# Aggregation in a written order for three engines, and three more units of it with split products

## The chip, the cores and the metric

The kernel runs on one core of a Trainium2 chip. The metric is device time in microseconds (us) from one execution; the time given for a kernel is the median of its runs. Engines are named as in the profile: PE is TensorE (matmuls; PEld its weight loads), DVE is VectorE, ACT is ScalarE, POOL is GpSimd, SP is SyncE. DMAs are issued from the queues of SP, ACT and POOL.

## The reference, cut to what matters

Two graph layers over N = 4096 nodes with D = 512 features, all in float32, one after the other:

```
bw, ba = sign(w0), max(sign(x), 0)
x  = layernorm(x + relu(adj @ (ba @ bw.T)))          # layer 0

h  = x @ edge_w
e  = where(adj > 0, h @ h.T, -9e15)
edge_att = softmax(e, axis=1)
node_att = softmax(x @ node_w, axis=0)
x  = layernorm(x + (adj * node_att * edge_att) @ (x @ w1) + bias)   # layer 1
```

## The kernel before, in words

The work runs in four stages, one after the other on PE.

**Layer 0** (from 0 to about 508 us) multiplies each block of 128 rows of `adj`, split into a high and a low part (`hi` on ACT, `lo` on DVE), with a packed product. The function `rest` then finishes one row block on DVE in steps that the main loop calls between the parts of the next row block. Every second row block, `rest` calls `left`, which combines two row blocks `low` and `high` of the new x into the seven left operands of a Strassen product and stores them in DRAM as `lop_d`, for the last stage.

**h and scores** (about 508 to 1075 us) compute `h` and `h @ h.T`, mask the scores, write them to DRAM as `s_d` and keep row minima and sums for the softmax.

**Aggregation** (from about 1075 us to the end) is where nearly all of the change lies. The product of the weighted attention with x is cut into 4 x 4 units `Aggregate(g, r)`: g is the block of output columns (1024 nodes), r the block of 1024 nodes that is summed over. A unit is one Strassen product: seven products m of a left operand (loaded from `lop_d`) with a right operand. The right operands are made of four tiles of 128 x 2048 elements: for each tile n the unit issues a load of the scores (`load`, POOL queue) and of `adj` (`mask`, POOL queue), then `shift` (DVE), `exp` (ACT), `clip` of adj (ACT), `weigh` (DVE, scores times adj), and after all four tiles four sums `combine` (DVE). Thirteen buffers of 1 MB (`slot`, `lent`) hold all of these; the list `free` gives them out.

One product m is either whole (two sums of 4 matmuls of 128 x 512 columns) or split once more into seven inner products (14 matmuls of 128 x 256 columns). Split are the three products m in `SPLIT` of the units for which `in_two(n)` holds, n = 4 to 14. The right operands of the inner products are made on DVE by `second` (four operations of 128 x 512 elements for a product) into one buffer, `extra[0]`; the left ones are made by `lefts` during the units n = 0 to 3 from the loaded `lop`, stored in DRAM as `lop2_d` from the ACT queue, and loaded by the later units in four DMAs for a product. Each sum lives in SBUF (`sums`) between units: ACT copies it into a PSUM bank (`seed`) and back (`evict`); there are six banks. At the end of a group g, `join_inner` and `join` (DVE) combine the products, and `Finish` multiplies them with w1 on PE (`po`, line 1244), adds them to x on DVE (line 1255), normalises and stores. The finishing of group g runs between the products of group g + 1, from the list `todo`, one entry for every 6 units of matmul work.

What sets the order of the aggregation: each unit has a list `steps()` of actions with a fraction of the unit of before it, at which an action is recorded. DVE's, ACT's and PE's instructions are then ordered by the scheduler of the programming layer, except those that are pinned with `keep_in_program_order`:

```python
    (0.53, lambda: (self.exp(2), self.shift(3))),
    (0.61, lambda: self.exp(3)),
    (0.63, lambda: self.clip(2)),
```

w1 is loaded into `w1_s` (line 1391, SP queue) before unit 0, and four DVE subtractions (`t3`, `r12`, `t2`, `t4`; line 1420) prepare it.

**The tail** (about 1901 us to the end) finishes the last group: `Finish` for its two halves, interleaved.

Of the kernel before, what the change touches and what calls it, by code (L numbers as in the profile page):

```python
# [11 lines left out]
F32 = mybir.dt.float32  # L12
# [12 lines left out]
SPLIT = 6, 4, 3  # L25
# [4 lines left out]
def kernel(  # L30
# [49 lines left out]

    lop2_d = [dram.tile([P, len(SPLIT), 4, BG // 2, P], F32, name=f"lop2_d{g}") for g in range(HG)]

# [76 lines left out]
    with (  # L159
# [153 lines left out]
        def rest(n, b, xb, acc, before):  # L313
# [4 lines left out]
            scr = wp.tile([P, D], F32, name="scr", tag="scr")  # L318
            nc.vector.scalar_tensor_tensor(xb, acc, 0.0, xb, ALU.max, ALU.add)
# [13 lines left out]
            if n % 2:  # L333
                left(n // 2, before, xb)
            yield
            transpose_rows(b, xb)

# [110 lines left out]
        def between_h(q, n):  # L448
            count[0] += q is None
            if q is None and count[0] % 14 in (8, 10, 13) and ahead_h:  # L450
                next(ahead_h.popleft())
            if q is None and count[0] > 6 and count[0] % 5 % 2 == 0:
                premask(nc.sync, 0, 3)
# [349 lines left out]
    panels = {}  # L803

    least = {}
# [6 lines left out]
    def panel(A):  # L812

        cols = slice(A * BG, (A + 1) * BG)
        nm = least.pop(A)
        pt = banks.popleft() if banks else ps_tr.tile([P, W], F32, name="ptm", tag="tr")
# [17 lines left out]
        d = small.tile([P, BG, NG], F32, name="d")  # L834
        nc.vector.tensor_tensor(d, nm.unsqueeze(2).to_broadcast([P, BG, NG]), nmax_c[:, cols, :], ALU.subtract)
        nc.scalar.activation(d, d, AF.Exp)
        nc.vector.tensor_mul(d, d, sum_c[:, cols, :])
        f = pan.tile([P, BG], F32, name="f")
# [4 lines left out]


    pinned = [tc.keep_in_program_order]

    class Aggregate:
# [58 lines left out]
        def steps(self):  # L906

            self.q, self.a, self.since = [None] * 4, [None] * 4, [None] * 8

            def begin():  # L910
                for n in range(2):
                    self.load(n)
                    self.mask(n)

            return [
                (0.0, begin),
                (0.14, lambda: self.load(2)),
                (0.15, lambda: self.shift(0)),
                (0.22, lambda: self.shift(1)),
                (0.25, lambda: self.exp(0)),  # L920
                (0.27, lambda: self.clip(0)),
                (0.28, lambda: self.load(3)),
                (0.30, lambda: self.exp(1)),
                (0.34, lambda: self.clip(1)),
                (0.36, lambda: self.weigh(0, 2, True)),
                (0.42, lambda: self.shift(2)),
                (0.47, lambda: self.weigh(1, 3, True)),
                (0.53, lambda: (self.exp(2), self.shift(3))),
                (0.61, lambda: self.exp(3)),
                (0.63, lambda: self.clip(2)),  # L930
                (0.68, lambda: self.weigh(2, None, True)),
                (0.71, lambda: self.clip(3)),
                (0.75, lambda: self.weigh(3, None, True)),
                *((0.8 + 0.05 * n, lambda n=n: self.combine(n)) for n in range(4)),
            ]

        def early_steps(self):
# [14 lines left out]
            for n in range(2):  # L952
                g = 2 * self.g + n
                yield lambda g=g: not rest[g], lambda g=g: (lowest(g), panel(g))
# [32 lines left out]
        def second(self, m):  # L987

            h, w = BG // 2, W // 2
            r = self.right(m)  # L990
            (r11, r12), (r21, r22) = [[r[:, k : k + h, c : c + w] for c in (0, w)] for k in (0, h)]
            t2, t3, t4 = (extra[0][:, n, :].rearrange("p (b w) -> p b w", w=w) for n in range(3))
            self.halves = r11, r21, r22, t4, r12, t2, t3
            nc.vector.tensor_sub(t3, r22, r12)
            nc.vector.tensor_sub(r12, r12, r11)
            yield
            nc.vector.tensor_sub(t2, r22, r12)
            nc.vector.tensor_sub(t4, r21, t2)
            yield

        def lefts(self, m, lop):

            (l11, l21), (l12, l22) = [[lop[:, k : k + 2, f : f + P] for f in (0, P)] for k in (0, BG // 2)]
            s = [rows.tile([P, 2, BG // 2, P], F32, name="left2", tag="rows") for _ in range(2)]
            s4, s3, s2, s1 = (x[:, n] for x in s for n in range(2))

            tc.keep_in_program_order(nc.vector.tensor_add(s1, l21, l22))
            tc.keep_in_program_order(nc.vector.tensor_sub(s2, s1, l11))
            tc.keep_in_program_order(nc.vector.tensor_sub(s3, l11, l21))  # L1009
            tc.keep_in_program_order(nc.vector.tensor_sub(s4, l12, s2))  # L1010
            to = lop2_d[self.r][:, SPLIT.index(m)]
            yield
            for n in range(2):
                nc.scalar.dma_start(to[:, ts(n, 2)], s[n])
# [5 lines left out]
        def main(self, between, two):  # L1020
            uses = deque(u for u in plan if u.unit is self)
            whole = sum(u.work for u in uses)
            halves = (None for m in [u.m for u in uses if u.ns and u.ns[0] == 1] for _ in self.second(m))
            stores = deque()
            past = 0
            while plan and plan[0].unit is self:
                u = plan.popleft()
                u.seed()
# [6 lines left out]
                if stores:  # L1035
                    next(stores.popleft(), None)
                if not u.ns:
                    next(halves, None)
                if u.end:
                    free.append(self.right(u.m))  # L1040
                    if not self.g and u.m in SPLIT:
                        stores.append(self.lefts(u.m, lops["lop"]))
                        next(stores[0])
                between(past / whole, u.work)
            if stores:
                next(stores.popleft(), None)
# [13 lines left out]
    class Sums:  # L1060
# [3 lines left out]
        lefts = 0, 1, 2, 6, 5, 4, 3  # L1064

        def __init__(self, unit, m, h=0, more=False, keep=False, ns=None):
# [5 lines left out]
            self.bank = None  # L1072

# [4 lines left out]
        def seed(self):  # L1078
# [8 lines left out]
            if self.unit.r:  # L1087
                assert self.ns or not any(m == self.m for m, _ in [*inner, *inner_next])
                nc.scalar.copy(self.bank[:, : self.w], self.to())  # L1089
            elif self.w < W:  # L1090
                nc.vector.memset(self.bank[:, : self.w], 0.0)

        def multiply(self):
            r, m = self.unit.r, self.m
            if self.begin and not self.ns:
                lops["lop"] = lopp.tile([P, BG, HD], F32, name="lop")
                nc.sync.dma_start(lops["lop"], lop_d[r][:, m])
            elif self.begin:
                low, high = (lopp.tile([P, 4, BG // 2, P], F32, name="lop2", tag="lop") for _ in range(2))
                raw, s = lop_d[r][:, m], lop2_d[r][:, SPLIT.index(m)]  # L1100
                nc.sync.dma_start(low[:, :2].rearrange("p n b f -> p (n b) f"), raw[:, :, :P])
                nc.sync.dma_start(low[:, 2:], s[:, :2])
                nc.sync.dma_start(high[:, :2], s[:, 2:])
                nc.sync.dma_start(high[:, 2], raw[:, BG // 2 :, P:])
                lops["low"], lops["high"] = low, high
            if self.ns:
                products = []
                for k, n in enumerate(self.ns):
                    at = self.lefts[n]
                    lop = lops["high"][:, at - 4] if at > 3 else lops["low"][:, at]  # L1110
# [3 lines left out]
            start = not r and self.w == W  # L1114
            for ps, lop, rop, K in products:
                for k in range(K):
                    nc.tensor.matmul(ps, lop[:, k, :], rop[:, k, :], start=start, stop=(k == K - 1), skip_group_check=True)  # L1117
                    start = False
            if self.keep:
                kept.append(self.bank)  # L1120

        def evict(self):
            u = self.unit
            if not self.keep:
                assert u.r or not self.ns or not any(m == self.m for m, _ in [*inner, *inner_next])
                nc.scalar.copy(self.to(), self.bank[:, : self.w])  # L1126
                banks.append(self.bank)
            if self.end and self.ns and (u.r == HG - 1 or blocks.index(u) == len(blocks) - 2):
                inner_next.extend((self.m, n) for n in range(7))
# [20 lines left out]
    def join_inner(g, m, n):  # L1150
# [4 lines left out]
        m1, m6, m7 = both[:, :w], both[:, w:], part(g, m, (6,))  # L1155
        out_, a, b = (
            (c11, m1, c11),
# [3 lines left out]
            (c22, m7, c22),  # L1161
            (c12, m6, c12),
            (c21, m7, c21),
        )[n]
        nc.vector.tensor_add(out_, a, b)

    def join(g, n, engine):
# [12 lines left out]
        engine.tensor_tensor(out_, a, b, op)  # L1180

    spare = []

    class Finish:

# [6 lines left out]
        def steps(self, then):  # L1192

            for q in range(2):
                yield from self.pair(q, ps_tr)
                some = q, q + 2
                yield lambda some=some: self.norm(some)
                yield lambda some=some: (self.scale(some), then and then.load(some))
# [12 lines left out]
        def pair(self, q, pool):  # L1211
# [6 lines left out]
            def combine():  # L1218
# [10 lines left out]
                nc.vector.tensor_sub(s2, l21, l11)  # L1229

            def multiply(name, lop, rop, *to):
# [11 lines left out]
                for k in range(KD // 2):  # L1243
# [7 lines left out]
                    )  # L1251
                f, _ = panels[self.A]
                for i, h in to:
                    xb = self.xbs[i][:, ts(h, HD)]
                    nc.vector.scalar_tensor_tensor(xb, po, f[:, i : i + 1], xb, ALU.mult, ALU.add)

# [10 lines left out]

            yield combine
            yield lambda: multiply("y", l11, 0, (a, 0))
            yield lambda: (multiply("x", l12, 1, (a, 0)), half_stats(a, 0))  # L1270
            yield lambda: multiply("y", 1, 5, (a, 1))
            yield lambda: (multiply("z", 0, 4, (b, 1)), nc.vector.tensor_sub(l12, l12, s[1]))
            yield lambda: (multiply("y", 2, 6, (b, 1)), half_stats(b, 1))
            yield lambda: (multiply("z", 3, 2, (a, 1)), half_stats(a, 1))
# [218 lines left out]
```

## Time and profile before

| | |
|---|---|
| median of 3 runs | 1931.44 us (1930.81 to 1933.38) |
| profiled execution, own time | 1934.05 us |
| its span, first to last instruction | 1932.3 us |
| PE busy | 1913.5 us, 99% of the span |
| DVE busy | 1387.0 us, 72% |
| ACT busy | 1024.3 us, 53% |
| POOL busy | 280.5 us, 15% |
| DMA | 508.72 MB, mean 263 GB/s |

Shares of busy time are averages over the stages; the stages have different limits, and a stretch of time is read by itself. In groups of instructions each row gives the line, engine, operation, output and inputs with their shape, the count, the busy time, the mean of one instruction in ns, and the idle time of the engine just ahead of it with what ended it. A matmul in float32 leaves two records in the trace.

### The profile page before, as it was taken

To read this page: it belongs to the slowest core of one execution; us is meant where nothing else is said; L and a number is where in the kernel's file an instruction comes from. 1 tells how busy PE (TensorE), PEld (TensorE's weight loads), DVE (VectorE), ACT (ScalarE), POOL (GpSimd) and SP (SyncE) were. 2 spreads that over 40 slices of the span, in tenths; PEclk is the share of its full clock that TensorE was granted. 3 is DMA by queue.
4 is the path that set the end of the run, shared out by engine and by line. 5 is a ranking of instruction groups with operands and counts; after the bars stand their busy time and mean duration, and the time that the engine had idled before them with its cause. 6 is when DMAs were issued, how large, how long until landed. Compare 5 with 4: busy or idle time off the path is not lost.

```text
span 1932.3 us, 20169 instructions
## 1 busy us (share of the span) xinstructions
PE 1913.5 (99%) x6708; PEld 1200.9 (62%) x6708; DVE 1387.0 (72%) x2058; ACT 1024.3 (53%) x1619; POOL 280.5 (15%) x409
## 2 busy tenths in 40 slices
PE   8999999999999999999999999999999999999998
PEld 6888888888644455444555444456666666666655
DVE  6766676666765567566664986687869987798746
ACT  5433333333202567576777665546767577757731
POOL 0122122222321101011111111111101101111100
PEclk9999999999999999999999999999999999999999
DMA  8888888888585478577773998787778787887731
GB/s 311 285 328 308 306 311 307 328 308 292 176 280 198 157 259 312 188 276 253 294 301 113 347 327 285 271 283 246 259 266 292 259 279 260 301 283 258 274 109 44
DMA packets 169527, 508.72 MB, mean 263 GB/s; under 512 B 15696, under 2 KB 41040, under 8 KB 161744
## 3 DMA queue, kind: packets, MB, share of 16 engines
q1 hardware_dynamic: 89472, 226.39, 34.6%
q0 software_dynamic: 64688, 239.10, 33.1%
q10 hardware_dynamic: 15264, 41.95, 6.0%
q8 instruction: 53, 0.87, 0.2%
q14 instruction: 50, 0.41, 0.1%
HBM read 385.74 MB, written 121.63 MB: 263 GB/s over the span
## 4 chain that ended last, share of the span: by engine, by line
PE 90%; DVE 4%; DMA 2%; issue 2%; ACT 1%; POOL 0%; ACTq 0%; DVEq 0%; POOLq 0%
PE bank L1117 33%; PE seven L749 14%; PE acc L395 11%; PE acc L396 11%; PE pe L676 6%; PE seven L101 5%; PE po L1244 3%; PE pt L638 3%; DMA slot<-s_d 1%; PE pt L355 1%; PE acc L236 1%; PE acc L235 1%; PE pw L213 1%; DMA over<-in_w_dram 1%; PE bank L1244 0%
## 5 line engine op out<-in xcount | busy, mean ns | idle before, releaser
L1117 PE MATMUL bank<-lent,lop 128*128 128x512 f32 (+1 forms) x1136 | 420.0, 517 | 0.0
L395 PE MATMUL acc<-xw,hi 128*128 128x512 f32 x960 | 376.5, 392 | 0.0
L396 PE MATMUL acc<-xw,lo 128*128 128x512 f32 x960 | 373.9, 390 | 0.0
L1117 PE MATMUL bank<-slot,lop 128*128 128x256 f32 (+1 forms) x1052 | 357.8, 488 | 1.9 <-DVE slot L898 1.9
L1117 PEld LDWEIGHTS bank<-lent,lop 128*128 128x128 f32 x1136 | 215.7, 190 | 173.9 <-issue 159.5
L1117 PEld LDWEIGHTS bank<-slot,lop 128*128 128x128 f32 x1052 | 200.2, 191 | 136.7 <-issue 116.6
L385 ACT CAST hi<-at 128x1024 fp32r<-128x1024 f32 x120 | 126.4, 1053 | 203.6 <-PE acc L395 152.9
L387 DVE TENSOR_TENSOR lo<-at,hi 128x1024 fp32r<-128x1024 f32 x120 | 148.0, 1233 | 85.7 <-ACT hi L385 85.7
L396 PEld LDWEIGHTS acc<-xw,lo 128*128 128x128 f32 x960 | 180.3, 188 | 36.8 <-DVE lo L387 0.3
L395 PEld LDWEIGHTS acc<-xw,hi 128*128 128x128 f32 x960 | 180.3, 188 | 36.8
L1126 ACT COPY over<-bank 128x512 f32<-128x512 f32 x200 | 115.0, 581 | 117.3 <-PE bank L1117 103.8
L676 PE MATMUL pe<-hT 128*128 128x512 f32 (+3 forms) x384 | 132.1, 486 | 0.0
L609 ACT ACTIVATE line<-line,nmax_c 128x512 f32<-128x512 f32 x160 | 114.8, 725 | 22.5 <-DVE nmax_c L600 22.3
L600 DVE CUSTOM_DVE_ANT_0 line<-lent,slot 128x512 f32<-128x512 bf16 x140 | 90.7, 688 | 47.7 <-ACT slot L686 26.7
L877 ACT ACTIVATE slot<-slot 128x2048 f32<-128x2048 f32 x36 | 68.8, 1911 | 73.6 <-DMA slot<-in_adj_t_dram 73.6
L871 DVE CUSTOM_DVE_ANT_1 lent<-lent,line 128x2048 f32<-128x2048 f32 x40 | 91.2, 2283 | 17.0 <-ACT line L831 8.6
L874 ACT ACTIVATE lent<-lent 128x2048 f32<-128x2048 f32 x40 | 76.5, 1913 | 49.1 <-DVE lent L871 49.0
L676 PEld LDWEIGHTS pe<-hT 128*128 128x128 f32 x384 | 64.6, 191 | 41.4 <-issue 33.8
L749 PE MATMUL seven<-hT 128*128 128x512 f32 x192 | 89.8, 593 | 0.0
L1089 ACT COPY bank<-over 128x512 f32<-128x512 f32 x144 | 84.7, 597 | 2.9 <-DVE left L1009 0.2
L638 PEld LDWEIGHTS pt<-ident,lent 128*128 128x128 f32 x418 | 52.3, 141 | 52.2 <-issue 38.3
L639 ACT COPY slot<-pt 128x512 f32<-128x512 f32 (+3 forms) x123 | 68.5, 560 | 22.9 <-PE pt L638 22.9
(261 smaller groups left out, 2828.2 us busy)
## 6 DMA issues: line engine op xcount, KB each, us to landing
at<-in_adj_t_dram SPq DMA_DIRECT2D x60, 1024.0 KB, 7.3
lop<-lop_d SPq DMA_DIRECT2D x79, 512.0 KB, 4.7
lent<-s_d POOLq DMA_DIRECT2D x39, 1024.0 KB, 7.3
slot<-in_adj_t_dram POOLq DMA_DIRECT2D x38, 1024.0 KB, 6.8
s_d<-slot POOLq DMA_DIRECT2D x30, 1024.0 KB, 7.2
lent<-in_adj_t_dram POOLq DMA_DIRECT2D x26, 1024.0 KB, 7.1
lop<-lop_d SPq DMA_DIRECT2D x99, 256.0 KB, 4.1
lent<-in_adj_dram SPq DMA_DIRECT2D x48, 512.0 KB, 5.0
```

Source lines behind the costliest of these rows:

```text
L101: nc.tensor.matmul(banks[bank][q], lop(m, q)[k], rop(m)[k], start=(first and k == 0), stop=(k == K - 1), skip_group_check=not first,)
L385: nc.scalar.copy(hi, aq)
L387: nc.vector.tensor_sub(lo, aq, hi.bitcast(F32))
L395: nc.tensor.matmul(acc, hi[:, c, :], xw[:, kb, :], start=(kb == 0), stop=False)
L396: nc.tensor.matmul(acc, lo[:, c, :], xw[:, kb, :], start=False, stop=(kb == NB - 1))
L609: nc.scalar.activation(line, line, AF.Exp, bias=nmax_c[:, b, c : c + 1], scale=-1.0, accum_out=sum_c[:, b, c : c + 1])
L638: nc.tensor.transpose(pt[:, j, :], src[:, ts(j, P)], ident)
L676: nc.tensor.matmul(pe[:, lo * P :], hT[:, k, ts(A * BG + i, P)], hT[:, k, (B * BG + lo) * P : (B + 1) * W], start=(k == 0), stop=(k == KD ...
L749: nc.tensor.matmul(ps, left[m][:, k, q, :], right[m][:, k, :], start=(first and k == 0), stop=(k == KD // 2 - 1), skip_group_check=not first,)
L871: pinned[0](nc.vector._custom_dve(TENSOR_ADD_SAT, out=q, in0=q, in1=m, s0=0.0, s1=-HUGE))
L1117: nc.tensor.matmul(ps, lop[:, k, :], rop[:, k, :], start=start, stop=(k == K - 1), skip_group_check=True)
L1126: nc.scalar.copy(self.to(), self.bank[:, : self.w])
```

## The change

1. `in_two(n)` becomes `0 < n`: the units n = 1 to 3 have three split products as well. For this the inner left operands are made in layer 0: `rest` starts a generator `lefts` for every second pair of row blocks, which loads what is needed from `lop_d` (POOL queue), makes the sums on DVE and stores `lop2_d` from the POOL queue. The old `lefts` in the aggregation goes. Unit 0 stays whole; when its three products in `SPLIT` are evicted, one DVE subtraction each turns the sum into the form that the inner products add to (`fresh` and the subtraction in `evict`).
2. A split product loads its left operands in two DMAs of 512 KB (`lop` and `inner`) instead of four.
3. `join_inner` takes five operations instead of seven, with two of them twice as wide.
4. In the whole aggregation DVE, ACT and PE run in the order in which the program issues them (`manual_schedule`). That order comes from four running clocks (`pe`, `dve`, `act`, `dma`), advanced by a written cost for each instruction (`spend`). A unit's loads, shifts, exps, clips, weighs and combines are `Step`s with predecessors; `fill` issues those that can start by a given time. Entries of `todo` carry a time from which they are ready.
5. The load of w1 moves from ahead of unit 0 to unit 1, its four subtractions to unit 2. `panel` is issued in three parts.

```diff
-SPLIT = 6, 4, 3
+SPLIT = 4, 6, 3
...
+            inner = n % 2 and n // 2 % BG > 1 and lefts(n // 2, xb)
...
             if n % 2:
                 left(n // 2, before, xb)
+            if inner:
+                next(inner)
             yield
             transpose_rows(b, xb)
+            if inner:
+                late.append(inner)
+                while n < NB - 1 and inner is not next(inner, inner):
+                    yield
+        def lefts(b, high):
+            to, of = lop2_d[b // BG][:, :, b % BG - 2], lop_d[b // BG][:, :, b % BG - 2, :]
+            low = wp.tile([P, len(SPLIT), HD], F32, name="low")
+            for k, m in ((slice(2), slice(4, 7, 2)), (2, 3)):
+                nc.gpsimd.dma_start(low[:, k, :], of[:, m, :])
+            for _ in range(3):
+                yield
+            for k, a, to_a in ((2, high[:, HD:], sums_l[:, 0, :]), (slice(2), sums_l[:, 1:4:2, :], None)):
+                to_a = a if to_a is None else to_a
+                (l11, l21), (l12, l22), (s4, s1) = ((x[..., :P], x[..., P:]) for x in (low[:, k, :], a, to_a))
+                nc.vector.tensor_add(s1, l22, l21)
+                nc.vector.tensor_sub(l21, l11, l21)
+                nc.vector.tensor_sub(l11, s1, l11)
+                nc.vector.tensor_sub(s4, l12, l11)
+                yield
+                nc.gpsimd.dma_start(to[:, k, :2], to_a.rearrange(...))
+            nc.gpsimd.dma_start(to[:, :, 2:], low.rearrange("p k (n f) -> p k n f", f=P))
...
+    clock = {"pe": 0.0, "dve": 0.0, "act": 0.0, "dma": 0.0}
+    def spend(engine, cost, ready=0.0):
+        clock[engine] = max(clock[engine], ready) + cost
+        return clock[engine]
...
+            if self.engine == "dma":
+                self.done = spend("dma", self.cost, clock["pe"]) + 4.0
+            else:
+                self.done = spend(self.engine, self.cost, self.ready())
...
+    def fill(until):
+        while True:
+            here = [x for x in pending if x.engine == "dma"][:1]
+            here = [x for x in here if x.can()]
+            if here:
+                emit(here[0])
+                continue
+            here = [x for x in pending if x.engine == "act" and x.can()]
+            here = [x for x in here if max(x.ready(), clock["act"]) + x.cost <= clock["pe"] + (0.43 * plan[0].work if plan else 3.4) + 1.2]
+            if here:
+                emit(min(here, key=lambda x: max(x.ready(), clock["act"])))
+                continue
+            here = [x for x in pending if x.engine == "dve" and x.can()]
+            if here and clock["dve"] < until:
+                soonest = max(clock["dve"], min(x.ready() for x in here))
+                if soonest < until:
+                    emit(next(x for x in here if x.ready() <= soonest))
+                    continue
+            break
...
+            loads = [Step("dma", 3.6, lambda n=n: self.load(n), ok=room) for n in range(4)]
+            masks_ = [Step("dma", 3.6, lambda n=n: self.mask(n), ok=room) for n in range(4)]
+            shifts = [
+                Step("dve", 2.29, lambda n=n: self.shift(n), [loads[n]], lambda n=n: 2 * self.g + n % 2 in panels)
+                for n in range(4)
+            ]
+            exps_ = [Step("act", 1.91, lambda n=n: self.exp(n), [shifts[n]]) for n in range(4)]
+            clips = [Step("act", 1.91, lambda n=n: self.clip(n), [masks_[n]]) for n in range(4)]
...
+        self.fresh = not unit.r or unit is blocks[1] and ns in ((0, 5), (6,))
...
+            if self.begin and self.ns:
+                lops["inner"] = lopp.tile([P, BG // 2, 4, P], F32, name="lop2", tag="lop")
+                nc.sync.dma_start(lops["inner"], lop2_d[r][:, SPLIT.index(m)])
...
+                if u is blocks[0] and self.end and self.m in SPLIT:
+                    upper, lower = (sums[:, 0, self.m, h, W // 2 :] for h in range(2))
+                    nc.vector.tensor_sub(upper, upper, lower)
...
-        return HG <= n < len(blocks) - 1
+        return 0 < n < len(blocks) - 1
...
-    nc.sync.dma_start(w1_s, w1.rearrange("(k p) o -> p k o", p=P))
...
+    order_ = {mybir.EngineType.DVE, mybir.EngineType.Activation, mybir.EngineType.PE}
+    with tc.manual_schedule(engines=order_):
+        for n, u in enumerate(blocks):
...
+            if n == 1:
+                nc.sync.dma_start(w1_s, w1.rearrange("(k p) o -> p k o", p=P))
+            elif n == 2:
+                for o, a, b in ((t3, r22, r12), (r12, r12, r11), (t2, r22, r12), (t4, r21, t2)):
+                    todo.append(Todo(lambda o=o, a=a, b=b: (nc.vector.tensor_sub(o, a, b), spend("dve", 0.69))))
...
+                if todo and not inner and not inner_next:
+                    owed[0] += work
+                    pace = max(4, ahead[0] / (len(todo) + 2))
+                    go = owed[0] >= pace and (todo[0].ready is None or todo[0].ready() <= clock["pe"])
+                    if go:
+                        owed[0] = min(owed[0] - pace, 2 * pace)
+                        fill(clock["pe"] + 1.1)
+                        todo.popleft()()
```

## The prediction

> **What bounds the kernel now.** I read the engine table by stage first, then who PE waits for, then single rows. In the table of windows the columns are the stretch, its length, and the busy time of PE, PEld, DVE, ACT and POOL with counts, the granted clock, the DMA share and GB/s:
>
> ```profile
> 60.00:430.00 370.00, 370.00 (x1682) 306.53 (x1681) 258.54 (x404) 122.04 (x151) 84.37 (x124) 1.00 0.85 309
> ...
> 1074.90:1121.00 46.10, 44.16 (x100) 19.26 (x100) 41.59 (x45) 26.10 (x34) 9.44 (x13) 0.96 0.97 357
> 1121.00:1169.00 48.00, 48.00 (x114) 21.21 (x113) 41.04 (x30) 33.06 (x34) 5.92 (x9) 1.00 0.92 330
> ...
> 1500.00:1700.00 200.00, 198.27 (x679) 127.75 (x678) 167.36 (x194) 135.89 (x176) 22.21 (x30) 1.00 0.78 271
> ```
>
> PE is busy throughout: 370.00 of 370 us in layer 0, 198.27 of 200 in the aggregation. DVE is second with 167 of 200 us, ACT third with 136. At the start of the aggregation DMA is nearly full (0.97). All that PE waits for from 1090 to 1900 us is this (total, times, longest):
>
> ```profile
> PE po L1244 <- DVE xb L1255: 4.0, 4, 1.7
> PE bank L1117 <- DVE slot L898: 1.9, 1, 1.9
> ```
>
> So the end moves only by PE's own work, by these 5.9 us, and by waits that the change adds. The price of PE's work I take from the spacing of rows, since the durations overlap:
>
> ```profile
> 1320.13 10.46 PE L1117 MATMUL bank<-slot,lop 128*128 128x512 f32 x24
> 1330.43 1.89 PE L1244 MATMUL po<-over 128*128 128x256 f32 x8
> 1332.16 1.89 PE L1117 MATMUL bank<-lent,lop 128*128 128x256 f32 x8
> 1333.88 1.03 PE L1117 MATMUL bank<-slot,lop 128*128 128x256 f32 x4
> ```
>
> From 1320.13 to 1330.43 are 24 records: 0.429 us for one of 512 columns; from 1332.16 to 1333.88 are 8: 0.215 us for one of 256.
>
> [...] the rows agree (24 records of 517 ns on average would be 12.4 us, they took 10.30), hence the spacing. [...] So what stands first in a written order holds up what is behind it; the next part shows it at 1085 us. [...]
>
> **The change part by part.**
>
> *PE work.* A whole product is 8 matmuls of two records: 16 x 0.429 = 6.87 us. Split it is 14 matmuls, 28 x 0.215 = 6.02 us. Three units with three such products gain 9 x 0.85 = **7.7 us**. The instruction lists of the two programs agree: 72 matmuls of 512 columns fewer, 126 of 256 more. PE is full there, so all of it lies on the path.
>
> *The wait at 1088 us.* DVE's row and PE's:
>
> ```profile
> 1084.96 0.69 DVE L1420 TENSOR_TENSOR line<-over 128x512 f32<-128x512 f32 x1 [4.48 <-DMA over<-in_w_dram]
> 1085.57 2.28 DVE L896 TENSOR_TENSOR slot<-slot,slot 128x2048 f32<-128x2048 f32 x1
> ...
> 1090.72 15.70 PE L1117 MATMUL bank<-slot,lop 128*128 128x512 f32 x32 [1.95 <-DVE slot L898]
> ```
>
> DVE stood 4.48 us before a subtraction of w1, the combines of unit 0 queued behind it, and PE ran out of right operands. In the new list the four combines follow each other (4 x 2.28 us from about 1080.5), the second is done near 1085 and PE wants it at 1088.7. w1 comes a unit later, its subtractions two. **-1.9 us**, and a margin of 3 us is next.
>
> *Waits of po for DVE*, 4.0 us in four places: PE multiplies with w1 while DVE has not yet read that bank. The new list holds such an entry until its clock says that DVE is done. I take half, **-2.0**; bounds 0 and -4.0.
>
> *DVE in the aggregation.* Added: `second` for nine products, 36 x 0.68 = 24.5 us, and `join_inner` for g = 0, 3 x (3 x 0.42 + 2 x 0.68) = 7.9. Removed: the old `lefts`, 48 x 0.42 = 20.1, and some 2.3 from the shorter joins of g = 1 to 3. With small ones (three subtractions after unit 0, three memsets, split panels) the list sums to 733 us instead of 720, beside 833 instead of 841 of PE: 88%. So DVE stays second. What matters is its margin at each handover. I added the row durations along each list, up to the operation that PE needs: at PE's first split product of unit 1, PE has 55.0 us of own work behind it, DVE 45.9. The smallest margin is 6.0 us, 3.5 us later (the old list had 10.5 in this stretch); by unit 2 it is 15, from unit 5 on over 28. DVE's waits for loads come out of that.
>
> *ACT* has 549 us in either list. Its exps and clips now stand between the evictions in a fixed place. *SP* loads two pieces of 512 KB for a split product (landing 4.6 us) where it loaded four; `inner` can start when the split product before is nearly done and is wanted 0.86 us into the next, with 6.9 us of a whole product between: 8 us against 4.6, hidden; one that took more than 8 us would cost its excess. *POOL* has the same 121 big loads. The old stores of `lop2_d` (24 DMAs on ACT's queue) are gone. For waits that the written order adds I take **+1.5 us**; bounds 0 and +13 (rival A). No row bounds it better, since this order is not in the trace.
>
> *Layer 0.* Eight times `lefts` adds four DVE operations of 128 and four of 256 columns, at most 8 x 8 x 0.42 = 27 us. They fall into two parts, each in one quarter row of 3.75 us. There DVE has gaps of 1.15 and 1.80 us while ACT makes `hi`; 4 x 0.42 = 1.7 fits nearly, and `hi` and `lo` have two buffers each: PE waited 0.3 us for `lo` in the whole stage. Behind the new waits on `low` stands the next `lo`; the load is issued three quarters (11 us) ahead and loads land in 7. POOL's queue gets 40 small DMAs of some 0.7 us (84 of 370 us busy now); a row block is stored from `scr` in time for its next use, 11 us later. One x load on SP moves past an adj load in every second pair and is issued by 111 us of its period, when the next adj load went out at 114: no wait. Traffic grows by about 9.4 MB on 139, the share from 0.85 to 0.91. The last two `lefts` fall into the start of h, where nine operations (3 us) stand in front of the adds that free PSUM banks, with 3 to 4 us of margin. **+0.6 us**; bounds 0 and +4.
>
> Sum: -7.7 - 1.9 - 2.0 + 1.5 + 0.6 = **-9.5 us**. The profiled execution took 1934.05 us (span 1932.3, 1.75 around it), so a like one would take 1924.5. The median of the runs is 2.6 below that; from it, 1931.44 - 9.5 = **1921.9 us**. A measurement of this kernel tells about 0.2%, 3.9 us, from no change.
>
> **The rivals.**
>
> *A, slower: ACT holds up the evictions.* Now ACT waits for adj tiles:
>
> ```profile
> ACT slot L877 <- DMA slot<-in_adj_t_dram: 73.6, 28, 8.1
> ...
> ACT lent L877 <- DMA lent<-in_adj_t_dram: 33.8, 17, 6.9
> ```
>
> 45 waits, up to 8.1 us, none of which reaches PE. If the clocks believe a load to land 7.6 us after issue (3.6 + 4.0) and it comes later, the clip stands in ACT's list ahead of the evictions and seeds, and with six banks PE stops. With a quarter of 45 waits costing PE 1.2 us: 13.5 instead of 1.5 and no gain at po, -7.7 - 1.9 + 13.5 + 0.6 = +4.5: 1935.9. It decides from 9.0 us of such waits. For it: DMA at 0.97 where margins are smallest, median landings of 6.8 to 7.4 us. Against it: the cost in the clocks is about what rows measure, and the margin grows.
>
> *B, no change: DVE is late in many small places.* Each of the 84 products with w1 before the tail has an exact place among PE's work; with 0.1 us at each (8.4) and po's gain gone: -0.6, 1930.8. Against it: DVE idles 12% and its costs are those of the rows.
>
> *C, all waits go:* -7.7 - 1.9 - 4.0 = -13.6: 1917.8.
>
> That the change doesn't do what it says (the nine products not split) is excluded by the counts of matmuls.
>
> **How the numbers follow.** Likeliest case 0.66, its own range 1918.5 to 1927; A 0.16; B 0.10; C 0.08. All but A and B are faster by over 0.2%, and A slower. The range of 1917.5 to 1931.5 leaves out most of A. Chances: faster 0.74, within 0.2% 0.10, slower 0.16.
>
> **What would show it.** In the profile after: PE's records of 256 columns up, the last matmul of the aggregation (1901 now) near 1892; no wait for a combine at the start; DVE's busy time in the aggregation up by some 13 us; waits of PE for L1255's like under 4 us; layer 0 ending within 1 us of 508. A list of PE waits on ACT's copies between banks and sums would make A true, many short ones on DVE B. A layer 0 that ends over 4 us later would mean that I took the new left operands too lightly.

## The result, and the profile after

The changed kernel takes 1927.93 us in the median of 20 runs (1926.69 to 1931.16), the kernel before 1932.51 (1930.56 to 1933.95, 20 runs): a ratio of 0.9978 with a 95% interval of 0.9971 to 0.9985. It is 4.6 us faster, where the prediction had 9.5. The profiled execution took 1931.16 us (span 1929.4) against 1934.05 (span 1932.3). It is the slowest of the 20: it lies 3.2 us above its median, and the one before 1.5 us above its own. So the profiles show 1.7 us less gain than the medians.

Read by stage, the gain and a loss stand apart. PE's first matmul of h starts at 516.01 us (before: 508.53), so layer 0 became **7.5 us longer**. h and the scores take as long as they did, 566.3 us. From there PE's last matmul comes 839.3 us later (849.7), so aggregation and tail became **10.4 us shorter**. 7.5 - 10.4 = -2.9 is the difference of the two profiled executions.

Windows of the kernel after, in the columns that the prediction explains. The second one still holds 7 us of the scores, since all has moved back by that much:

```profile
60.00:430.00 370.00, 365.46 (x1650) 302.06 (x1649) 268.69 (x442) 119.67 (x149) 105.53 (x151) 0.99 0.88 321
1074.90:1121.00 46.10, 45.71 (x125) 22.11 (x124) 40.41 (x45) 29.94 (x49) 8.17 (x11) 1.00 0.92 337
1500.00:1700.00 200.00, 199.81 (x685) 128.94 (x684) 173.33 (x197) 131.18 (x178) 23.24 (x31) 1.00 0.79 283
```

In the aggregation PE is busy 199.81 of 200 us, with DVE at 173: as forecast. In layer 0, where PE had no gap at all, 4.5 us are missing now. PE's waits from 60 to 1900 us (total, times, longest) say for what:

```profile
PE acc L424 <- DVE lo L415: 4.5, 1, 4.5
PE bank L1186 <- DMA lop<-lop_d: 2.3, 1, 2.3
PE seven L779 <- ACT lent L810: 0.7, 1, 0.7
PE bank L1186 <- DVE slot L967: 0.6, 1, 0.6
PE pt L668 <- ACT lent L716: 0.4, 1, 0.4
PE bank L1186 <- ACT bank L1159: 0.2, 1, 0.2
```

The four waits of `po` (4.0 us) and the one for a combine (1.9 us) are gone. Two new ones have come: one of 4.5 us in layer 0 and one of 2.3 us for a left operand. (The 0.7 and 0.4 us lie in the scores.)

**The 4.5 us, followed back.** PE's rows, then DVE's, then POOL's, start and duration first, the idle time and its releaser in brackets:

```profile
81.14 0.47 PE L423 MATMUL acc<-xw,hi 128*128 128x512 f32 x1
86.15 0.79 PE L424 MATMUL acc<-xw,lo 128*128 128x512 f32 x1 [4.54 <-DVE lo L415]
86.74 0.63 PE L423 MATMUL acc<-xw,hi 128*128 128x512 f32 x1
87.17 0.63 PE L424 MATMUL acc<-xw,lo 128*128 128x512 f32 x1
```
```profile
84.26 0.69 DVE L327 CUSTOM_DVE_ANT_0 scr<-xb,nw_b 128x512 f32<-128x512 f32 x1 [5.54 <-DMA x_d<-scr]
84.88 0.08 DVE L327 DVE_READ_ACCUMULATOR2_ANT node_s<- 128x1 f32 x1
84.88 1.22 DVE L415 TENSOR_TENSOR lo<-at,hi 128x1024 fp32r<-128x1024 f32 x1
```
```profile
69.02 0.74 POOL L376 DMA_DIRECT2D lop_d<-xb  x1 [3.06 <-DVE xb L326]
77.00 0.57 POOL L352 DMA_DIRECT2D low<-lop_d  x1 [7.25 <-DMA lop_d<-xb]
77.57 0.54 POOL L332 DMA_DIRECT2D x_d<-scr  x1
```

PE waits for `lo`. `lo` is late because DVE stands 5.54 us in front of L327, which writes `scr`, until the store of the last row block out of `scr` has been read. That store is issued at 77.57 us, 5 us later than before (72.52), because POOL has an issue of `low<-lop_d` ahead of it, and that load reads what the store at 69.02 writes: POOL stands 7.25 us until it has landed.

The first DVE operation on this `low` comes at 146.96 us, 70 us after the load. In layer 0 only DVE and ACT are in a written order; POOL's instructions are placed by the scheduler, and it moved the load up in POOL's list, to where its operand exists.

**What a gap costs beyond its length.** Windows of the kernel after, the granted clock third from last:

```profile
82.00:86.00 4.00, 0.00 (x0) 0.00 (x0) 1.74 (x3) 0.95 (x2) 0.00 (x0) 0.79 1.03 407
86.00:88.00 2.00, 1.85 (x4) 1.49 (x5) 2.00 (x4) 0.00 (x0) 1.62 (x3) 0.50 1.01 385
88.00:90.00 2.00, 2.00 (x6) 1.59 (x5) 1.10 (x2) 0.00 (x0) 0.99 (x2) 0.50 0.93 277
90.00:92.00 2.00, 2.00 (x7) 1.56 (x7) 0.00 (x0) 0.01 (x1) 0.12 (x1) 0.71 0.81 236
92.00:94.00 2.00, 2.00 (x12) 1.67 (x11) 0.93 (x1) 1.52 (x2) 0.00 (x0) 1.00 0.95 301
```

Behind the gap PE runs at half clock: 86.74 to 87.17 is 0.43 us for a record, where the rows ahead of the gap (79.65, 79.88, 80.10) are 0.23 apart. From 86 to 92 us that loses 2 x 0.50 + 2 x 0.50 + 2 x 0.29 = 2.6 us. With the wait, 4.5 + 2.6 = 7.1 of the 7.5 us.

The wait at 1088 us in the kernel before had the same tail, which I had not read. Its windows, with PE back at 1090.72 us:

```profile
1090.00:1092.00 2.00, 1.28 (x2) 0.77 (x3) 2.00 (x3) 2.00 (x3) 0.00 (x0) 0.70 1.02 387
1092.00:1094.00 2.00, 2.00 (x3) 0.69 (x3) 2.00 (x3) 0.27 (x1) 0.00 (x0) 0.50 1.02 393
1094.00:1096.00 2.00, 2.00 (x6) 0.81 (x5) 2.00 (x2) 0.00 (x0) 1.50 (x2) 0.94 1.02 393
```

2 x 0.30 + 2 x 0.50 + 2 x 0.06 = 1.7 us more: that wait was worth 1.9 + 1.7 = 3.7 us. So is the new wait of 2.3 us at 1717 us (clock 0.58 and 0.56 from 1719 to 1723): 2 x 0.42 + 2 x 0.44 = 1.7.

### The profile page after: what moved, and what is told of

Read it like the earlier page. It is cut to its first block, busy times and chain, and to the rows that moved or that the text cites. A ratio compares the mean times of both kernels' runs of the same rounds, so it can differ in the third digit from the quotient of the medians.

```text
span 1929.4 us, 20429 instructions
## 1 busy us (share of the span) xinstructions
PE 1908.7 (99%) x6816; PEld 1224.0 (63%) x6816; DVE 1436.1 (74%) x2113; ACT 1023.3 (53%) x1647; POOL 309.5 (16%) x449
## 4 chain that ended last, share of the span: by engine, by line
PE 93%; DVE 3%; DMA 2%; ACT 1%; issue 0%; ACTq 0%; POOL 0%; DVEq 0%
PE bank L1186 36%; PE seven L779 15%; PE acc L424 11%; PE acc L423 11%; PE pe L706 5%; PE seven L101 5%; PE po L1336 4%; PE pt L668 3%; PE acc L236 1%; PE acc L235 1%; PE pt L383 1%; PE pw L213 1%; DMA lop<-lop_d 1%; PE bank L1336 0%; DVE slot L955 0%
## 5 line engine op out<-in xcount | busy, mean ns | idle before, releaser
L1186 PE MATMUL bank<-lent,lop 128*128 128x256 f32 (+1 forms) x1496 | 483.1, 473 | 0.1
L1186 PEld LDWEIGHTS bank<-lent,lop 128*128 128x128 f32 x1496 | 284.2, 190 | 166.9 <-issue 140.1
L1186 PE MATMUL bank<-slot,lop 128*128 128x512 f32 (+1 forms) x800 | 288.1, 506 | 3.1 <-DMA lop<-lop_d 2.3
L1186 PEld LDWEIGHTS bank<-slot,lop 128*128 128x128 f32 x800 | 152.6, 191 | 118.0 <-issue 104.0
L1348 DVE SCALAR_TENSOR_TENSOR xb<-po,f,xb 128x256 f32<-128x256 f32 x84 | 40.3, 481 | 73.6 <-PE po L1336 73.6
```

## The experiments

Each was timed beside the kernel before, and the ratio is to that; rows and stages are of its profiled execution, and h begins at PE's first matmul of h. Letters in the expectations are of theories as they stood then. **T**: layer 0 pays for the `low` load that stands ahead of the store of `scr` on POOL's queue, not for the work on DVE or the traffic that `lefts` adds. **H**: a wait of PE costs its length and then a stretch of half clock.

**1. Load kept in its place.** All else as in the kernel after:

```diff
-                nc.gpsimd.dma_start(low[:, k, :], of[:, m, :])
+                tc.keep_in_program_order(nc.gpsimd.dma_start(low[:, k, :], of[:, m, :]))
```

> The changed kernel with the two loads of low pinned at their place in POOL's order, so that the first no longer stands ahead of a store of scr. Theory T (one load on POOL waits 7.25 us for a store of lop_d, the store of scr is behind it, DVE waits for that store, PE waits 4.5 us for lo and then runs some 5 us at half clock): h begins at 508.5 to 509.5 us instead of 516.0, the time is 7.2 us under the changed kernel's 1927.9, about 1920.7, ratio to before 0.994. Rival R (the work that was added to layer 0, on DVE, POOL and DMA, costs the time): h still begins after 514, time 1926 or more.

Measured: 1921.6 us (before 1933.05), ratio 0.9936 (0.9922 to 0.9949). POOL's and DVE's rows at the same place:

```profile
68.89 0.74 POOL L376 DMA_DIRECT2D lop_d<-xb  x1 [3.07 <-DVE xb L326]
72.51 0.57 POOL L332 DMA_DIRECT2D x_d<-scr  x1 [2.88 <-DVE scr L331]
```
```profile
78.80 0.69 DVE L327 CUSTOM_DVE_ANT_0 scr<-xb,nw_b 128x512 f32<-128x512 f32 x1
79.42 0.08 DVE L327 DVE_READ_ACCUMULATOR2_ANT node_s<- 128x1 f32 x1
79.42 1.22 DVE L415 TENSOR_TENSOR lo<-at,hi 128x1024 fp32r<-128x1024 f32 x1
```

The store goes out at 72.51 us, L327 waits for nothing, PE loses nothing, and h begins at 508.75. The first `low` load is issued at 131.4 us. All DVE work and all traffic of `lefts` is still there, so these cost layer 0 some 0.2 us at most (508.75 against 508.53). This version beats both kernels.

**2. The store on another queue.** The load stays where it was too early; only the store moves:

```diff
-            nc.gpsimd.dma_start(x1_d[ts(b, P), :], scr)
+            nc.sync.dma_start(x1_d[ts(b, P), :], scr)
```

> The changed kernel with the store of scr issued from SP's queue instead of POOL's; the loads of low stay early in POOL's order and still wait there. T: the store is no longer behind the load, DVE and PE do not wait, h begins near 508.5 to 510, time about 1920.7, unless SP now holds up its adj loads for the store (then up to a few us more, seen as waits for adj). R2 (any long wait of the load on POOL costs the time, by the stores of lop_d behind it): h begins near 516, time 1928.

Measured: 1921.13 us, ratio 0.9935 (0.9922 to 0.9949). POOL, then SP:

```profile
76.73 0.59 POOL L352 DMA_DIRECT2D low<-lop_d  x1 [7.35 <-DMA lop_d<-xb]
```
```profile
71.96 0.33 SPq L332 DMA_DIRECT2D x_d<-scr  x1
```

POOL still waits 7.35 us, but h begins at 508.44 us: nothing is lost by it. It is not the wait that costs, but the store that stood behind it.

**3. Layer 0's part alone.** The kernel before with `lefts` in layer 0, its stores going to a buffer that nothing reads:

```diff
+            inner = n % 2 and n // 2 % BG > 1 and lefts(n // 2, xb)
...
+            to, of = lop3_d[b // BG][:, :, b % BG - 2], lop_d[b // BG][:, :, b % BG - 2, :]
```

> The kernel before with the layer 0 part alone: it loads low, makes the inner left operands on DVE and stores them to a DRAM tensor that nothing reads; the aggregation stays as before. The outputs are as before. T: POOL's order has the same load ahead of the same store, so h begins near 516 and the time is 7.2 us over before, 1939.7, ratio 1.0037. Rival R3 (the loss belongs to the written order of the aggregation): time within 1 us of before.

Measured: 1939.21 us, ratio 1.0031 (1.0018 to 1.0044): 6.2 us slower. h begins at 515.88 us (+7.4), with the same wait of PE:

```profile
PE acc L425 <- DVE lo L416: 4.4, 1, 4.4
```

The loss in layer 0 comes with this part of the change and needs no other. Aggregation and tail took 3.5 us less here than in the kernel before (846.2 against 849.7), though DVE's and PE's lists there are in the same order: the waits of `po` were 2.8 us instead of 4.0, and the wait for the second combine was 1.6 us, without half clock behind it. So the waits of one order can differ by that much between two executions.

**4. The written order without the nine products.** As 1, with `in_two` and `fresh` as before:

```diff
-        return 0 < n < len(blocks) - 1
+        return HG <= n < len(blocks) - 1
```

> As the first of these (loads pinned), but only the units n = 4 to 14 have split products, as before: the written order alone, without the 7.7 us of PE work. T: against before it gains the 1.9 us at 1088 and the 4.0 us of po, and loses 0 to 3.5 us to the new waits that the changed kernel shows (2.3 for a load of lop, 0.8 for others): 1926.6 to 1930.1, ratio 0.997 to 0.999. Rival R4 (the order gains nothing, all gain is matmul work): 1931 or more.

Measured: 1927.58 us, ratio 0.997 (0.9959 to 0.9982). Aggregation and tail take 842.9 us: 6.8 less than before. The waits that left sum to 3.7 + 4.0 = 7.7, those that came to 1.1. Against 1 (837.3) the nine products are worth 5.6, or 7.3 if one takes off that 1 has 1.7 us more of waits (2.8 against 1.1): near the 7.7 of the sum.

**5. The nine products without the written order.** As 1, with the aggregation left to the scheduler:

```diff
-    with tc.manual_schedule(engines=order_):
+    if True:
```

> The kernel with pinned loads of low (1921.6), but the aggregation's DVE, ACT and PE instructions are left to the scheduler of the programming layer: nine more split products without the written order. Theory O (the written order is worth the waits that it takes away): PE waits again for po or combines, 4 to 12 us of waits with half-clock time behind the longer ones; time 1926 to 1934. Rival (matmul work alone counts, any order will do): 1921 to 1924.

Measured: 1941.57 us, ratio 1.0047 (1.0032 to 1.0062): 20 us slower than 1, and slower than expected. PE's waits:

```profile
PE po L1336 <- DVE xb L1348: 4.3, 2, 3.9
PE bank L1186 <- ACT bank L1159: 4.1, 3, 2.2
PE bank L1186 <- DVE slot L982: 3.9, 1, 3.9
```

With 0.5 us for a load these are 12.8 us, 10.0 more than in 1. Behind three of them the clock is 0.50 for 6.8, 3.4 and 6.8 us; PE is busy for 14.0 us of that, which loses 7.0. Together this is 17.0 of the 18.8 us by which aggregation and tail are longer than in 1 (856.1 against 837.3); the rest I did not find. So in this order the nine products do not pay. But it is not the order of the kernel before with nine products more: there the four combines of unit 0 are pinned, and here they are not. The wait for L982 comes from that. A shift stands between the first combine and the second, and DVE waits in front of it:

```profile
1089.25 2.29 DVE L955 CUSTOM_DVE_ANT_1 lent<-lent,line 128x2048 f32<-128x2048 f32 x1 [4.06 <-PE bank L1186]
```

What nine products would cost or gain in a scheduler's order with these pins, no run shows.

**6. w1's load ahead of unit 0 again**, with one subtraction ahead of unit 0's combines, to see the wait at 1088 us come back:

```diff
+    nc.sync.dma_start(w1_s, w1.rearrange("(k p) o -> p k o", p=P))
...
+                nc.vector.tensor_sub(t3, r22, r12)
+                spend("dve", 0.69)
                 for x in u.combining((), (), (), ()):
```

> The kernel with pinned loads, but w1 is loaded ahead of unit 0 and its first subtraction stands ahead of the combines of unit 0, as in the kernel before; the other three subtractions stay in unit 2. Theory H (a wait of PE of some 2 us costs as much again, since PE's granted clock is 0.50 for some 3.6 us after it): PE waits 1.9 to 2.1 us near 1089, its clock falls to 0.5 behind, and the aggregation is 3.5 to 4.0 us longer than with pinned loads: 1925.3. Rival (a wait costs its own length): 2.0 us longer, 1923.6.

Measured: 1922.18 us, ratio 0.9946 (0.9933 to 0.996). DVE stood 4.08 us for w1, PE only 1.1, and the clock stayed at 1.00. With so short a wait the run says nothing on H. Runs 7 and 8 make the wait longer.

**7 and 8. As 6, with all four subtractions there, and with the first two**, which makes one wait of PE, of known cause, at the same place:

```diff
-                nc.vector.tensor_sub(t3, r22, r12)
-                spend("dve", 0.69)
+                for o, a, b in ((t3, r22, r12), (r12, r12, r11), (t2, r22, r12), (t4, r21, t2)):
+                    nc.vector.tensor_sub(o, a, b)
+                    spend("dve", 0.69)
```

> The kernel of e1 (1921.6 us) with the load of w1 ahead of unit 0 and all four subtractions of w1 ahead of unit 0's combines, so that PE meets a wait of known place and cause near 1088 us. DVE stood 4.08 us for w1 with one subtraction ahead (then PE waited 1.1 us); three more of 0.69 us make the wait 2.9 to 3.2 us. Theory H (a PE wait of over about 2 us costs its own length and then some 1.8 us more, because the granted clock is halved behind it): PEclk near 0.50 for 3 to 5 us behind the wait, and the aggregation 4 to 5 us longer than with e1: 1925.5 to 1926.5 us. Rival (a wait costs its own length alone): PEclk stays at 1.00, the aggregation 2 to 3 us longer, 1923.5 to 1924.5.

> As e9, with only two subtractions of w1 ahead of unit 0's combines: the wait near 1088 us should be 1.7 to 1.9 us. Theory H with a limit near 2 us: PEclk stays at 1.00 behind it, the aggregation 1 to 1.8 us longer than with e1, 1922.5 to 1923.5 us; if it is halved here too, as it was behind the 1.95 us of the kernel before, 3 to 3.7 us longer, near 1925. Rival: as long as its wait, whatever the clock: 1922.5 to 1923.5 too; so the reading is the PEclk behind the wait and the spacing of the records there.

Measured: four, 1926.55 us, ratio 0.9967 (0.9954 to 0.998); two, 1923.22 us, 0.9951 (0.9937 to 0.9965). With four, PE's row and the windows behind it:

```profile
1092.00 2.92 PE L1186 MATMUL bank<-slot,lop 128*128 128x512 f32 x3 [3.08 <-DVE slot L982]
```
```profile
1090.00:1092.00 2.00, 0.00 (x0) 0.00 (x0) 1.97 (x2) 0.08 (x1) 0.00 (x0) 0.81 1.02 387
1092.00:1094.00 2.00, 2.00 (x3) 0.96 (x4) 2.00 (x1) 2.00 (x2) 0.00 (x0) 0.50 1.03 393
1094.00:1096.00 2.00, 2.00 (x4) 0.87 (x3) 1.97 (x2) 0.30 (x1) 1.16 (x2) 0.50 1.02 393
1096.00:1098.00 2.00, 2.00 (x3) 0.66 (x2) 2.00 (x2) 0.00 (x0) 0.33 (x1) 0.50 1.03 391
```

With two:

```profile
1090.72 3.70 PE L1186 MATMUL bank<-slot,lop 128*128 128x512 f32 x8 [1.86 <-DVE slot L982]
```
```profile
1090.00:1092.00 2.00, 1.28 (x3) 0.68 (x4) 1.97 (x2) 0.00 (x0) 0.00 (x0) 1.00 1.02 387
1092.00:1094.00 2.00, 2.00 (x6) 0.93 (x5) 1.97 (x2) 1.81 (x1) 0.45 (x1) 1.00 1.02 391
```

The wait is 1.2 us longer with four (3.08 against 1.86), but aggregation and tail 4.0 us (842.4 against 838.3; the medians are 3.3 apart). The other 2.8 are the half clock: 3 x 2 x 0.50 = 3.0. H is shown for a wait of 3.08 us, and the rival, that a wait costs its length alone, is refuted there; behind 1.86 us there is no half clock. Against 1 both runs are some 0.6 us longer than their waits and clock explain; what that is I did not find.

**9. The wait for a left operand at 1717 us.** SP's queue there has a load of `xb` that waits for stores, and the loads of `lop` are behind it. Run 1 still waited 1.0 us for such a load. In this run, as 1, the load of `xb` comes one entry of `todo` later:

```diff
-                yield Todo(lambda some=some: (self.scale(some), then and then.load(some)), lambda: self.normed)
+                yield Todo(lambda some=some: self.scale(some), lambda: self.normed)
+                yield Todo(lambda some=some: then and then.load(some))
```

> The kernel with pinned loads, but the loads of the next rows of x stand one entry of todo later than the stores into the same buffers that they wait for. Theory S (SP's queue stands up to 9 us at these loads, and a load of lop behind them comes late once, PE waits 1.0 us near 1711): no wait of PE for lop, time 1920 to 1921.5. Rival (the load of lop is late because the DMA engines are full there, 0.97): the wait stays, time unchanged within 0.5 us.

Measured: 1921.39 us, ratio 0.9942 (0.9929 to 0.9954), no different from 1. A wait of 1.3 us for a left operand is left, at another place (1388 us). But the edit did not take away what S blames: SP still stands up to 8.8 us at the loads of `xb` (8.0 in run 1). So the run does not decide between S and its rival. The waits were 2.3, 1.0, 0.7 and 0.2 us in the kernel after and runs 1, 2 and 4, and each time, as in this run, PE waited for one of the first two loads of `lop` behind those of `xb`. These landed 12.0, 9.5, 9.2 and 9.9 us after their issue (6.5 here), where the median is 4.3 to 4.6. What made them land so late stays open.

**10. What the clocks' load time is worth.** As 1, with loads believed to land later:

```diff
-                self.done = spend("dma", self.cost, clock["pe"]) + 4.0
+                self.done = spend("dma", self.cost, clock["pe"]) + 8.0
```

> The kernel with pinned loads, but the clocks believe that a load lands 8.0 us after its share of the DMA engines instead of 4.0, so that DVE's and ACT's work on a tile stands later in the order. If loads that land later than the clocks believe are what remains (PE waits 1.6 us for L967 near 1724, 1.0 for lop): these get shorter, time 1919 to 1921. If the order has little room because DVE is 87% busy: work crowds up ahead of the handovers, PE waits for combines and for second, time 1924 to 1935.

Measured: 1926.42 us, ratio 0.9967 (0.9955 to 0.9979): 4.8 us slower than 1. PE's waits:

```profile
PE bank L1186 <- DVE slot L967: 3.2, 2, 2.4
PE bank L1186 <- DVE lent L1083: 2.6, 3, 1.8
```

Here the more careful figure made a worse order. As I read it, DVE's operations on loaded tiles are put later in its list, so that it comes late to the weighs (L967) and to `second` (L1083) that PE needs; which move does it was not taken apart. At 4.0 (plus 3.6 of transfer) rival A's worry, loads that come later than the clocks believe, did not come true: PE waited 0.2 us for ACT's copies.

## Why the prediction was wrong in size, point by point

The sign and the mechanism in the aggregation were right. The failed step is layer 0.

| term | predicted | measured | from |
|---|---|---|---|
| PE work, nine products | -7.7 | -7.3 | runs 1 and 4 |
| wait at 1088 us | -1.9 | -3.7 | the wait and its half clock |
| `po` | -2.0 (0 to -4.0) | -4.0 | no such wait after |
| new waits of the written order | +1.5 (0 to +13) | +4.8 | 2.3 + 0.6 + 0.2, and 1.7 of half clock |
| layer 0 and handover | +0.6 (0 to +4) | +7.5 | start of h |

The four terms of the aggregation were -10.1 and sum to -10.2; measured directly it is -10.4. Three of them were off, and cancel: that the sum fits is luck.

The measured column is of the two profiled executions, which are 2.9 us apart, not 4.6 as the medians are. By medians layer 0 costs 6.3 to 6.8 us (1927.93 against runs 1 and 2). The new waits are probably smaller in most runs too: 16 of the 20 have a mean clock of 0.998 (the profiled one 0.997), which leaves at most 9.6 us at half clock. The profiled one had 6.8 us in layer 0 and 3.4 us behind the wait at 1717 us; those 16 cannot have had both. Nor is the wait at 1088 us worth 3.7 us in every execution: in run 3 the same wait was 1.6 us.

**Layer 0, the failed step.** The term was +0.6 us and measured +7.5. The prediction said that "a row block is stored from `scr` in time for its next use, 11 us later", and that behind the waits on `low` "stands the next `lo`". The first took POOL's list for the order of the program. In that order the load comes at 131 us (run 1 shows it there), two pairs of row blocks after the data that it reads; in the list that ran it came at 77 us, ahead of the store of `scr`, and 70 us ahead of its use instead of the "three quarters (11 us)" of the prediction. I had followed what is queued behind the new wait on DVE, and had counted POOL's DMAs without reading what stands behind them on POOL. The gap alone, 4.5 us, is over the upper bound of +4, and the half clock behind it was in no term. What the prediction named as the sign of this error, a layer 0 that ends over 4 us later, is what came. Runs 1 and 2 each take the whole loss away by taking one of the two DMAs out of the other's way, and run 3 brings it back on its own. Without it the change gives 1921.6, where 1921.9 was forecast. That is closer than the reasoning was: against the kernel before, timed beside it, run 1 gains 11.4 us (1933.05 to 1921.6), and the prediction without its layer 0 term had 10.1.

**The wait at 1088 us** went for the reason given. The four combines follow each other, the second is done at 1092.6, and PE's row of 34 records runs through without a wait:

```profile
1087.99 2.29 DVE L980 TENSOR_TENSOR slot<-slot,slot 128x2048 f32<-128x2048 f32 x1
1090.31 2.29 DVE L982 TENSOR_TENSOR slot<-slot,slot 128x2048 f32<-128x2048 f32 x1
```
```profile
1085.77 14.76 PE L1186 MATMUL bank<-slot,lop 128*128 128x512 f32 x34
```

Its size was taken from the wait alone. The windows of before had the 0.70 and 0.50 behind it; in the one window that I showed (46 us, clock 0.96) 4% of 46 us, 1.8 us, stood already.

**`po`**: I took half, without a reason against the whole. The entries wait for their clock, and no wait is left; in the scheduler's order (run 5) 4.3 us of them are back.

**New waits**: not where rival A had them. Of ACT's copies there are 0.2 us. DVE is late once, by 0.6 us, not in many places as in rival B. The one that costs is a load of `lop` on SP, 512 KB. The prediction found it hidden as long as it takes less than 8 us, with 4.6 us for the landing. This one was issued at 1707.05 us and landed 12.0 us later; DMA was full (share 1.03 from 1714 to 1717):

```profile
1706.00 0.95 SPq L1298 DMA_DIRECT2D xb<-x_d  x2
1707.05 1.38 SPq L1169 DMA_DIRECT2D lop<-lop_d  x1
```

No load of `lop` was issued from 1697.5 to 1707.05, because SP stood 8.5 us at the load of `xb` until a store had read that buffer:

```profile
SPq L1298 <- DMA out_dram<-xb: 8.7, 2, 8.5
```

So the landing was mis-sized, and SP's stand was in no term. How much of the wait comes from each is open (run 9).

**DVE** in aggregation and tail: the groups of instructions sum to 740 us against 722.5, +17.5 where the lists gave +13 (without the tail 690.8 against 677.1, +13.7). It hid as forecast: DVE held PE up once ahead of the tail, for 0.6 us.

## What to carry to other kernels

A DMA on a queue that nobody orders by hand was placed here by the scheduler, 54 us earlier than in the program; it read DRAM just written, so it waited 7.25 us in its queue, and everything behind it waited too. So read each queue's list in order, and ask for every wait what is behind it and which buffer that frees; pin such a load where it is needed, or give the store behind it another queue. And price a wait of PE of some 2 us or more with the half clock that may follow it: 1.7 to 3.0 us here, behind waits of 1.95 to 4.54 us.

## What the runs showed of the hardware that I had not expected

The half clock comes in stretches of one length or twice that. If the part of each window below full clock is taken at 0.50, the stretch behind the wait at 1088 us in the kernel before is (2 x 0.30 + 2 x 0.50 + 2 x 0.06) / 0.5 = 3.4 us, at 1719 us in the kernel after (2 x 0.42 + 2 x 0.44) / 0.5 = 3.4, in its layer 0 (4 x 0.21 + 2 x 0.50 + 2 x 0.50 + 2 x 0.29) / 0.5 = 6.8, and in run 7 likewise 6.8 (0.81, three times 0.50, then 0.99 over 4 us). The waits of PE ahead of the two short stretches were 1.95 and 2.31 us, ahead of the two long ones 4.54 and 3.08 us. The length of a wait does not decide alone: 1.86 us (run 8), 1.81 and 2.35 us (run 10, at 1270 and 1831 us) left the clock at 1.00. The longest of these, PE's row and the windows around it:

```profile
1833.98 1.55 PE L1186 MATMUL bank<-slot,lop 128*128 128x512 f32 x3 [2.35 <-DVE slot L967]
```
```profile
1831.00:1834.00 3.00, 0.65 (x3) 0.02 (x1) 3.00 (x3) 0.48 (x1) 0.00 (x0) 1.00 0.96 348
1834.00:1836.00 2.00, 2.00 (x5) 1.03 (x6) 2.00 (x1) 0.00 (x0) 0.00 (x0) 1.00 0.71 272
1836.00:1838.00 2.00, 2.00 (x6) 0.81 (x5) 1.97 (x2) 0.28 (x1) 0.00 (x0) 1.00 0.01 2
```

What else decides, for a wait of some 2 us, was not shown: no run changed the place of one wait and kept its length.
